# Causal self-attention in a decoder layer: the far corner of the transposed weights is moved by transfers, and its outputs contract over 128 keys

## The chip, the cores and the metric

The kernel runs on one core of a Trainium2 chip. The metric is device time in microseconds from launch to the last instruction, the median of three runs. The engines are TensorE (PE, with its weight loads shown apart as PEld), VectorE (DVE), ScalarE (ACT), GpSimd (POOL) and SyncE (SP), which here only issues DMA transfers.

## What is computed

A decoder layer on `x` of shape (2, 1024, 256) in fp32, with a layer norm after each of three parts: causal self-attention with 16 heads of 64 and rotary positions, cross-attention to a context of 77 tokens, and a feed-forward part that a router gives half of the tokens. The change concerns the first.

```python
q, k, v = rope(split(x @ Wq)), rope(split(x @ Wk)), split(x @ Wv)
sim  = einsum('bid,bjd->bij', q, k) * 64**-0.5
attn = softmax(where(tril, sim, -inf), axis=-1)
out  = einsum('bij,bjd->bid', attn, v)          # joined over heads, then @ Wo + bo
x    = layernorm(x + out)
# cross-attention, layernorm; gated feed-forward, layernorm
```

## The kernel before

**Tiling.** The 1024 tokens are `NT = 8` tiles of 128, and `NH = 4` is half of them. Two heads of 64 make a pair (`j` = 0, 1), and 2 batches times 8 pairs give 16 objects of class `Pair`. A score tile has 128 queries on the partitions and up to 1024 keys along the row, the causal part alone. Query tiles are worked in five groups, `(3, 1, 0), (4, 2), (5,), (6,), (7,)`.

**Steps of a pair**, named by letters in a hand-written order: `P` projections and `E` their copies out of PSUM; `d` (swap by DMA through `begin`, L219), `c`, `s`, `a` the rotation of half of the tokens, on POOL; `w` writes v to DRAM and `l` brings it back; `S` scores of a group (L342); `T` scale, mask and minimum on DVE (L355); `X` the exponentials on ACT (L363); `R` the transposes on DVE (L372); `Q`, `I`, `D`, `B` the inverse sums, sent through DRAM and spread along the row (`over`); `V0` to `V7` the outputs, one step per key tile (L410); `O` copies of the outputs out of PSUM (L424, for the last pair L430 with the scaling); `M` the scaling on POOL (L433); `W` the store. A step like `R41` is group 4, head 1.

**Transposes and outputs.** DVE transposes within blocks of 32 x 32. After step `R`, partition 32r + i of `p_t` holds key i of a block of 32, for the queries 32r to 32r + 31 of a tile: the partitions of quarter r still belong to query quarter r, and only the 32 partitions within a quarter run over keys. An output matmul can therefore contract only over 32 keys at a time: for key tile n, key block k of 4, head j and quarter r it takes 32 rows of `v4` (v arranged so that each partition quarter holds all keys in blocks of 32) and 32 rows of `p_t`, and adds into `po[r]`. Four quarters by two heads make eight tiles of 32 x 64 that work side by side in the array. Key tile n has 8 - n query tiles, so the columns of a matmul fall from 256 (V0) to 32 (V7).

**v.** `kept` copies both halves of v into one tile, `spread` writes all eight token tiles to `v_d` in DRAM, and `copies` reads them back into `v4` four times, once per quarter, on the queues of SP and ACT.

**Order.** TensorE, VectorE and ScalarE follow the order of three lists: `opening`, the periodic `steps` and `ending`. In a steady period the outputs of one pair lie among the scores of the next: `R40`, `S0`, `V0`, `V1`, `S1`, `V2` to `V4`, `S2`, `V5` to `V7`, `S3`. Scores have two PSUM buffers of two banks, one per head of a group, so `S` of a group waits for `T` of the group before it. SP issues in the order in which the text calls `begin`. After `V1` and `V7` the next `begin` waits for that output's last matmul (`gate`). Transfers from SP and ACT share eight completion semaphores in turn, and a transfer waits until the one eight places before it has landed.

**Pieces.** `split` cuts some projections into four column pieces and some scores into two, as many per pair as the list `pieces` allows. What is computed does not depend on it.

**Constants** (`causal`, `ones`, `earlier`, `b2`, `w_r`) are made or loaded at the start or after a `W` and kept throughout. `ones`, `earlier`, `b2` and `w_r` are used in the router and feed-forward part.

Of the kernel before, what the change touches and what calls it, by code (L numbers as in the profile page):

```python
# [8 lines left out]
F32 = mybir.dt.float32  # L9
# [7 lines left out]
P, R32 = 128, 32  # L17
B, T, C = 2, 1024, 256
H, D = 16, 64
# [3 lines left out]
NT = T // P  # L23
# [7 lines left out]
MASKED = -1e30  # L31
# [3 lines left out]
def decoder_layer(  # L35
# [23 lines left out]
    nc = tc.nc  # L59
    V, A, G, TE = nc.vector, nc.scalar, nc.gpsimd, nc.tensor  # L60

    const = ctx.enter_context(tc.tile_pool(name="const", bufs=1))
# [3 lines left out]
    dram = ctx.enter_context(tc.tile_pool(name="dram", bufs=2, space=DRAM))  # L66
# [14 lines left out]
    causal = const.tile([P, P], F32)  # L81
    make_causal_mask(nc, causal, MASKED)
    neg_half = const.tile([P, 1], F32)
    G.memset(neg_half, -0.5)
    ones = const.tile([P, P], F32)
    G.memset(ones, 1.0)
    earlier = const.tile([P, P], F32)
    make_upper_triangular(nc, earlier, diag=False)
# [42 lines left out]
    b2 = const.tile([P, C], F32)  # L131
    b_r = const.tile([P, 1], F32)
    b1 = const.tile([P, NF], F32)
    w_r = const.tile([P, C], F32)
# [7 lines left out]
    K4 = T // R32  # L142
    early = ctx.enter_context(ExitStack())
    e1 = early.enter_context(tc.tile_pool(name="early1", bufs=1, side="right"))
    e2 = early.enter_context(tc.tile_pool(name="early2", bufs=2, side="right"))
    with (
# [9 lines left out]
        fence = s1.tile([P, T], F32, name="fence")  # L156
        G.memset(fence[:, : T - P], 0.0)
        G.tensor_copy(fence[:, T - P :], causal)
        wo = s1.tile([P, NP, C], F32, name="wo")

        p_t = s1.tile([P, (NT + 1) * NT, P], F32, name="pT")
# [4 lines left out]
        def load(t, src):  # L166
            return lambda: nc.sync.dma_start(t, src)


        def load_next(h):  # L170
            if h == 0:
# [10 lines left out]
            3: [load(b2, L0_ffn_b2.partition_broadcast(P)), load(b_r, L0_ffn_b_r.partition_broadcast(P))],  # L182
            4: [
                load(w_r, L0_ffn_w_r.rearrange("c o -> (o c)").partition_broadcast(P)),
# [7 lines left out]
        NH = NT // 2  # L192
# [24 lines left out]
        def begin(dst, src):  # L217

            ins = nc.sync.dma_start(dst, src)  # L219
            if gate:  # L220
                tc.add_manual_dep(ins.ins, gate.pop().ins.name, after, reason="the outputs' instructions come first")
# [6 lines left out]
        pieces = [2, 1, 13, 13, 11, 10, 11, 12, 13, 12, 8, 9, 8, 8, 9, 0]  # L228
# [17 lines left out]
        class Pair:  # L246
# [61 lines left out]
            def kept(self, n):  # L308
                if self.v is None:
                    self.v = e1.tile([P, NT, P], F32, tag="v", name="v")  # L310
                    self.v_d = dram.tile([4, R32, NT * P], F32, tag="v", name="v_d")
                A.copy(self.v[:, n : n + NT // 2, :], self.pp["v", n])

            def spread(self):

                begin(self.v_d.rearrange("r k e -> (r k) e"), self.v.rearrange("p n d -> p (n d)"))

            def copies(self):

                self.v4 = s1.tile([P, K4, P], F32, tag="v4", name="v4")  # L320
                for r in range(4):
# [46 lines left out]
            def turn(self, g, j):  # L368
                for t, span in self.spans[g]:
                    first = (t, NT * (t + 1))[j]  # L370
                    step = (NT, 1)[j]
                    V.transpose(  # L372
                        p_t[:, first : first + t * step + 1 : step, :],
                        self.p[g, j][:, span].rearrange("p (n k) -> p n k", k=P),
                    )

# [22 lines left out]
            def output(self, n):  # L399
                if n == 0:  # L400
                    self.po = [ring.tile([P, NT, R32], F32, tag="t", name="po_self") for _ in range(4)]
                for k in range(4):
                    for j in range(2):
                        first = (NT * n + n, NT * (n + 1) + n)[j]
                        step = (1, NT)[j]
                        last = first + (NT - 1 - n) * step + 1

                        for r in range(k if n == NT - 1 else 0, 4):
                            rows = slice(r * R32, (r + 1) * R32)
                            ins = TE.matmul(  # L410
                                self.po[r][j * D : (j + 1) * D, n:, :],
                                self.v4[rows, NT * k + n, j * D : (j + 1) * D],
                                p_t[rows, first:last:step, k * R32 : (k + 1) * R32],
                                start=(n == 0 and k == 0), stop=(n == NT - 1 and k == r),
                            )
                if n in (1, NT - 1) and self.n < len(keys) - 1:
                    gate[:] = [ins]
                elif n == NT - 1:
                    final[:] = [ins]
# [20 lines left out]
        class Closing:  # L440
# [51 lines left out]
            ("Eq0", 1), ("Ek0", 1), ("Ev4", 1), ("Eq1", 1), ("a0", 0), ("R40", -1), ("S0", 0), ("T00", 0), ("T01", 0),  # L492
# [21 lines left out]
            "S": lambda a, x: a.scores(int(x)),  # L514
            "T": lambda a, x: a.least(int(x[0]), int(x[1])),
# [17 lines left out]
            0X31 0R20 1s0 0R30 0R21 1a0 2Eq1 0T40 3L 2Pv4 0T41 2Pv0 0X40 0X41 2Ek0 0R31 0R40 2Pq0 2Ev4 1S0 0R41 1T00  # L533
            2Eq0 2Ev0 0V0 1T01 0V1 2d0 0V2 1S1 1T11 0V3 1X00 0V4 0V5 1T10 1S2 1X01 1X11 1R00 0V6 0V7 2w 1X10 0O0 1T20
            1T21 1S3 1R10 1R01 0O1 2c0 1l 1X20 1T31 2Pk1 0O3 1T30 0O2 3Pv4 0Q 2Ek1 1S4 2c1 1X30 2s0 1X21 3Pq1 1R20 3Ev4
            3Pv0 2a0 1R11 3Pk0 0I 1T41 2d1 1R30 1X31 3Pq0 1T40 2S0 1R21 1X41 1X40 1R31 1R40 0D 1R41 2T00 3Ek0 2s1 3Eq1
# [7 lines left out]
            14S4 15Ek1 14T40 12W 4C 14T41 14X41 13O2 14R10 15a0 15d1 14R31 13O3 14R30 13D 14X40 15c1 14R40 14R41 15S0 4Y  # L544
# [3 lines left out]
            6U 15R41 15V0 4Z 14B 5Y 15V1 15V2 0f 15V3 14M 1f 7C 15V4 15V5 5Z 6Y 15V6 6Z 15D 15V7 15B 2f 15O1 15O3 7U 0n  # L548
# [8 lines left out]
        done, last = set(), len(keys) - 1  # L557
# [106 lines left out]
    def pool(name, bufs, **more):  # L664
        return ctx.enter_context(tc.tile_pool(name=name, bufs=bufs, reuse_waits="tile", **more))

    c1 = pool("cross1", 1)
# [5 lines left out]
    vo_d = dram.tile([B, HS, C], F32, tag="vo", name="vo_d", bufs=1)  # L673

# [86 lines left out]
    rows = out.rearrange("b t c -> (b t) c")  # L761
# [253 lines left out]
    with tc.manual_schedule(engines={TE.engine, V.engine, A.engine}):  # L1015
        first = Prepare()
# [139 lines left out]
```

## Time and profile before

| | us |
|---|---|
| median of 3 runs | 810.68 |
| lowest and highest run | 808.66, 815.99 |
| the profiled execution | 809.84 |
| its span, first to last instruction | 808.07 |
| self-attention with its rotation, from 51 to 526 of the span: PE busy | 462.7 of 475.0 |
| in that stretch DVE, ACT, POOL busy | 355.5, 254.1, 243.0 |
| 590 to 750 (cross-attention): PE busy | 159.4 of 160.0 |

The profile is one execution. A group line names the source line, engine and operation, then out<-in with their shapes and the count; then busy time, the mean in ns of one, and the idle time just before it with what ended that. A timeline line has start, length, line and operation, and in brackets the idle time before it. In a stage window the stretch comes first, then its length and each engine's busy time. PE's matmuls in fp32 run in two passes, so one matmul of the program is two rows of the trace. The granted clock of PE was 0.998 over the span.

### The profile page before, as it was taken

The numbers are of one execution on the slowest core, as the hardware profiler recorded it, in microseconds if no ns is written. First come the engines' busy times: TensorE is split into PE (matmuls) and PEld (weight loads), VectorE is DVE, ScalarE is ACT, GpSimd is POOL, SyncE is SP. The second block draws the span as 40 slices with busy tenths as digits, with TensorE's granted clock in tenths as the row PEclk, the third lists the DMA queues.
The fourth block names the chain that finished last, engine by engine and source line by source line (L and its number), as shares of the span: only waits on it lengthen the run. The fifth ranks groups of instructions, "written<-read, shape, count | busy, mean of one in ns | idle before, by whom it ended". The sixth has DMA issues, their size and how long they took to land.

```text
span 808.1 us, 26591 instructions
## 1 busy us (share of the span) xinstructions
PE 781.5 (97%) x11428; PEld 622.0 (77%) x11428; DVE 581.9 (72%) x1345; ACT 355.4 (44%) x842; POOL 367.7 (45%) x261
## 2 busy tenths in 40 slices
PE   8999999999999999999999988999999999999986
PEld 5565888888888888788788776688788888886745
DVE  2578678868778868678667796535577788888674
ACT  2565565655565556454554544102433332333130
POOL 2634455555375565365473553222033222261664
PEclk9999999999999999999999999999999999999999
DMA  5455477557567567668366467690450000011221
GB/s 195 129 148 177 129 210 209 171 168 211 157 169 230 158 179 223 174 171 204 112 198 185 133 185 158 173 324 3 168 187 1 1 1 0 1 53 53 68 91 52
DMA packets 65328, 112.32 MB, mean 139 GB/s; under 512 B 6497, under 2 KB 43707, under 8 KB 65211
## 3 DMA queue, kind: packets, MB, share of 16 engines
q1 hardware_dynamic: 59067, 89.64, 37.6%
q10 hardware_dynamic: 4608, 16.78, 7.5%
q0 software_dynamic: 1536, 4.20, 1.4%
q8 instruction: 90, 1.47, 0.8%
q14 instruction: 27, 0.22, 0.1%
HBM read 71.24 MB, written 22.59 MB: 116 GB/s over the span
## 4 chain that ended last, share of the span: by engine, by line
PE 82%; DVE 7%; POOL 4%; issue 4%; ACT 1%; DMA 1%; POOLq 0%; SPq 0%; ACTq 0%; DVEq 0%
PE po_self L410 17%; PE ps_scores L342 16%; PE pp_kq L268 13%; PE pp_v L303 7%; PE po_cross L998 6%; PE ps_cross L946 6%; PE po_proj L477 6%; PE pp_h L889 3%; PE po_ffn L900 2%; PE pt_p L978 1%; DVE pT L372 1%; DMA turned<-raw 1%; POOL comp L831 1%; POOL e L967 1%; DVE p L355 1%
## 5 line engine op out<-in xcount | busy, mean ns | idle before, releaser
L363 ACT ACTIVATE p<-p,neg 128x768 f32<-128x768 f32 (+7 forms) x256 | 196.3, 768 | 162.9 <-DVE neg L355 161.3
L355 DVE CUSTOM_DVE_ANT_0 p<-ps_scores,fence 128x512 f32<-128x512 f32 (+7 forms) x256 | 179.4, 750 | 104.9 <-PE ps_scores L342 104.5
L372 DVE STREAM_TRANSPOSE pT<-p 128x512 f32<-128x512 f32 (+7 forms) x256 | 175.7, 740 | 6.2 <-PE po_self L410 3.0
L410 PE MATMUL po_self<-pT,v 32*64 32x256 f32 (+6 forms) x7808 | 157.6, 295 | 10.1 <-issue 7.2
L410 PEld LDWEIGHTS po_self<-pT,v 32*64 32x64 f32 x7808 | 137.2, 130 | 34.9 <-issue 25.4
L342 PE MATMUL ps_scores<-kq 64*128 64x256 f32 (+3 forms) x1060 | 148.9, 411 | 1.8 <-DVE neg L355 1.0
L342 PEld LDWEIGHTS ps_scores<-kq 64*128 64x128 f32 x1060 | 93.3, 186 | 42.7 <-issue 28.2
L268 PE MATMUL pp_kq<-xT,w_pair 128*128 128x256 f32 (+2 forms) x524 | 118.6, 379 | 1.1 <-ACT xT L203 0.7
L291 POOL TENSOR_TENSOR turned<-turned,sin 128x1024 f32<-128x1024 f32 x31 | 73.2, 2362 | 93.0 <-DMA turned<-raw 80.1
L288 POOL TENSOR_TENSOR kq<-raw,cos 128x1024 f32<-128x1024 f32 x31 | 73.6, 2374 | 84.4 <-ACT raw L276 84.4
L268 PEld LDWEIGHTS pp_kq<-xT,w_pair 128*128 128x128 f32 x524 | 88.3, 190 | 23.9 <-issue 10.4
L967 POOL TENSOR_TENSOR e<-e,inv 128x616 f32<-128x616 f32 x32 | 38.2, 1215 | 113.0 <-DVE inv L966 67.2
L120 POOL TENSOR_TENSOR rs<-ve,neg_half 128x1 f32<-128x1 f32 x48 | 27.2, 570 | 107.2 <-DVE ve L118 105.2
L295 POOL TENSOR_TENSOR kq<-kq,turned 128x1024 f32<-128x1024 f32 x31 | 73.5, 2371 | 1.4
L998 PE MATMUL po_cross<-packed,pT 128*128 128x256 f32 (+1 forms) x320 | 72.5, 380 | 0.1
L946 PE MATMUL ps_cross<-wqk,x1T 128*128 128x308 f32 x256 | 69.2, 423 | 0.0
L998 PEld LDWEIGHTS po_cross<-packed,pT 128*128 128x128 f32 (+1 forms) x320 | 60.0, 190 | 9.4 <-ACT pT L984 0.3
L303 PEld LDWEIGHTS pp_v<-w_pair,xT 128*128 128x128 f32 x512 | 61.1, 192 | 4.0 <-issue 2.5
L303 PE MATMUL pp_v<-w_pair,xT 128*128 128x128 f32 x512 | 62.2, 275 | 0.0
L946 PEld LDWEIGHTS ps_cross<-wqk,x1T 128*128 128x128 f32 x256 | 47.4, 190 | 16.2 <-issue 0.7
L959 ACT ACTIVATE e<-e 128x616 f32<-128x616 f32 x32 | 23.0, 717 | 80.8 <-DVE e L955 80.8
L477 PE MATMUL po_proj<-wo,attnT 128*128 128x256 f32 x224 | 51.4, 381 | 0.3 <-ACT out_pair L424 0.3
(128 smaller groups left out, 817.0 us busy)
## 6 DMA issues: line engine op xcount, KB each, us to landing
turned<-raw SPq DMA_DIRECT2D x64, 256.0 KB, 4.7
v<-v_d ACTq DMA_DIRECT2D x32, 512.0 KB, 6.2
v<-v_d SPq DMA_DIRECT2D x32, 512.0 KB, 11.1
v_d<-v SPq DMA_DIRECT2D x16, 512.0 KB, 4.6
over<-inv_d SPq DMA_DIRECT2D x32, 256.0 KB, 4.8
attn_d<-out_pair SPq DMA_DIRECT2D x14, 512.0 KB, 4.3
attnT<-attn_d SPq DMA_DIRECT2D x8, 512.0 KB, 5.4
vo_d<-vo SPq DMA_DIRECT2D x2, 1232.0 KB
```

The lines of the kernel that those rows point to most:

```text
L268: TE.matmul(pp[:, cols], self.w[:, c, "kq".index(of), :], x_ts[self.b, n][:, c, cols], start=(c == 0), stop=(c == NC - 1),)
L288: E.tensor_tensor(self.kq[:, :, n * NB : (n + 1) * NB], self.raw[n], self.twice(cos, n), ALU.mult)
L295: E.tensor_tensor(dst, dst, self.turned[n], ALU.add)
L303: TE.matmul(pv[:, i, :], x_ts[self.b, 2 * n // NT][:, c, toks], self.w[:, c, 2, :], start=(c == 0), stop=(c == NC - 1),)
L342: TE.matmul(self.ps[j][:, cols], self.kq[rows, 1, t * P : (t + 1) * P], self.kq[rows, 0, cols.start - at : cols.stop - at], start=True, st ...
L355: V.tensor_tensor_reduce(p[:, span], self.ps[j][:, span], fence[:, T - (t + 1) * P :], -SCALE, -MASKED, ALU.add, ALU.min, neg[:, i : i + 1],)
L363: A.activation(p[:, span], p[:, span], AF.Exp, bias=neg[:, i : i + 1], scale=-1.0, accum_out=self.sums[:, j, t : t + 1],)
L372: V.transpose(p_t[:, first : first + t * step + 1 : step, :], self.p[g, j][:, span].rearrange("p (n k) -> p n k", k=P),)
L410: ins = TE.matmul(self.po[r][j * D : (j + 1) * D, n:, :], self.v4[rows, NT * k + n, j * D : (j + 1) * D], p_t[rows, first:last:step, k * R ...
L477: TE.matmul(self.po, of, wo[:, c, :], start=(c == 0), stop=(c == NP - 1))
L946: TE.matmul(ps[:, g, : Q * S], self.x_t[:, c, :], wqk[:, c, self.b, h : h + Q, :].rearrange("p h s -> p (h s)"), start=(c == 0), stop=(c = ...
L998: TE.matmul(po, self.p_t[:w, k, :], packed[self.b][:w, k, :], start=(k == 0), stop=(k == NK - 1))
```

## The change

`p_t` is laid out by key block of 32 first, so that the transposes of a tile go to four places with runs of 32 elements. A new step `J` comes after the last transposes of a pair: 16 transfers copy the weights of key tiles 4 to 7 and query tiles 4 to 7 (the far corner: under a causal mask key tiles 4 to 7 have no other queries) into `far`, such that partition quarter k gets key block k of every query quarter r. There the 128 partitions are 128 keys. The outputs V4 to V7 then contract over 128 keys at once: 8 matmuls of 128 rows by 64 columns per key tile, which take v directly from the copy of the projection (`self.v[NH]`), in place of 32 of 32 rows (20 for V7). Only key tiles 0 to 3 of v go through DRAM. `pieces` is zero for all pairs after the first. `causal` is made in place in `fence`; `ones`, `earlier`, `b2` and `w_r` move to the cross-attention stage.

```diff
-        pieces = [2, 1, 13, 13, 11, 10, 11, 12, 13, 12, 8, 9, 8, 8, 9, 0]
+        pieces = [2, 0, 0, 0, 0, 0, 0, 0, 0, 0, 0, 0, 0, 0, 0, 0]
...
-    K4 = T // R32
+    K4 = T // R32 // 2
...
-        p_t = s1.tile([P, (NT + 1) * NT, P], F32, name="pT")
+        p_t = s1.tile([P, 4, (NT + 1) * NT, R32], F32, name="pT")
+        far = s1.tile([P, 4, NT // 2 + 1, NT // 2, R32], F32, name="far")
...
             def kept(self, n):
                 if self.v is None:
-                    self.v = e1.tile([P, NT, P], F32, tag="v", name="v")
-                    self.v_d = dram.tile([4, R32, NT * P], F32, tag="v", name="v_d")
-                A.copy(self.v[:, n : n + NT // 2, :], self.pp["v", n])
+                    self.v = {}
+                self.v[n] = e1.tile([P, NH, P], F32, tag=f"v{n}", name="v", bufs=(1, 3)[n // NH])
+                A.copy(self.v[n], self.pp["v", n])
...
             def spread(self):
-                begin(self.v_d.rearrange("r k e -> (r k) e"), self.v.rearrange("p n d -> p (n d)"))
+                self.v_d = dram.tile([4, R32, NH * P], F32, tag="v", name="v_d")
+                begin(self.v_d.rearrange("r k e -> (r k) e"), self.v[0].rearrange("p n d -> p (n d)"))
...
                     V.transpose(
-                        p_t[:, first : first + t * step + 1 : step, :],
-                        self.p[g, j][:, span].rearrange("p (n k) -> p n k", k=P),
+                        p_t[:, :, first : first + t * step + 1 : step, :].rearrange("p c n q -> p n c q"),
+                        self.p[g, j][:, span].rearrange("p (n c q) -> p n c q", c=4, q=R32),
                     )
+
+            def joined(self):
+                for k in range(4):
+                    for r in range(4):
+                        begin(
+                            far[k * R32 : (k + 1) * R32, r, :, :, :].rearrange("p m t q -> p m (t q)"),
+                            p_t[r * R32 : (r + 1) * R32, k, NH * NT :, :].rearrange("p (m t) q -> p m (t q)", t=NT)[:, :, NH * R32 :],
+                        )
...
             def output(self, n):
...
+                if n < NH:
+                    for k in range(4):
+                        for j, cols in enumerate(heads):
+                            for r in range(4):
+                                rows = slice(r * R32, (r + 1) * R32)
+                                ins = TE.matmul(
+                                    self.po[r][cols, n:, :], self.v4[rows, NH * k + n, cols],
+                                    p_t[rows, k, across(j, n, NT), :], start=(n == 0 and k == 0), stop=False,
+                                )
+                else:
+                    for r in range(4):
+                        for j, cols in enumerate(heads):
                             ins = TE.matmul(
+                                self.po[r][cols, n:, :], self.v[NH][:, n - NH, cols],
+                                far[:, r, :, :, :].rearrange("p m t q -> p (m t) q")[:, across(j, n - NH, NH), :],
+                                start=False, stop=(n == NT - 1),
                             )
...
-            ("Eq0", 1), ("Ek0", 1), ("Ev4", 1), ("Eq1", 1), ("a0", 0), ("R40", -1), ("S0", 0), ("T00", 0), ("T01", 0),
+            ("Eq0", 1), ("Ek0", 1), ("Ev4", 1), ("Eq1", 1), ("a0", 0), ("R40", -1), ("J", -1), ("S0", 0), ("T00", 0), ("T01", 0),
...
-            6U 15R41 15V0 4Z 14B 5Y 15V1 15V2 0f 15V3 14M 1f 7C 15V4 15V5 5Z 6Y 15V6 6Z 15D 15V7 15B 2f 15O1 15O3 7U 0n
+            6U 15R41 15J 15V0 4Z 14B 5Y 15V1 15V2 0f 15V3 14M 1f 7C 15V4 15V5 5Z 6Y 15V6 6Z 15D 15V7 15B 2f 15O1 15O3 7U 0n
...
+    ones = c1.tile([P, P], F32, name="ones")
+    G.memset(ones, 1.0)
+    earlier = c1.tile([P, P], F32, name="earlier")
+    make_upper_triangular(nc, earlier, diag=False)
+    b2 = c1.tile([P, C], F32, name="b2")
+    w_r = c1.tile([P, C], F32, name="w_r")
+    nc.sync.dma_start(w_r, L0_ffn_w_r.rearrange("c o -> (o c)").partition_broadcast(P))
+    nc.sync.dma_start(b2, L0_ffn_b2.partition_broadcast(P))
```

`J` stands in the other two lists likewise, after `R41` of its pair.

## The prediction

> **What bounds the kernel now.** I read the busy times and the costliest groups first. PE is busy for nearly the whole span, and its largest line is the output matmuls of self-attention, L410.
>
> ```profile
> PE 781.5 (97%) x11428; PEld 622.0 (77%) x11428; DVE 581.9 (72%) x1345; ACT 355.4 (44%) x842; POOL 367.7 (45%) x261
> L410 PE MATMUL po_self<-pT,v 32*64 32x256 f32 (+6 forms) x7808 | 157.6, 295 | 10.1 <-issue 7.2
> ```
>
> The share is an average, so next comes PE's timeline of one steady period. Pairs of heads follow each other every 29.8 us (in the chain of waits the first score blocks start at 259.37 and 289.20). The order is S0, V0 V1, S1, V2 V3 V4, S2, V5 V6 V7, S3 and then projections.
>
> ```profile
> 259.30 1.80 PE L342 MATMUL ps_scores<-kq 64*128 64x256 f32 x20
> 261.03 3.50 PE L410 MATMUL po_self<-pT,v 32*64 32x256 f32 x128
> 264.46 2.00 PE L342 MATMUL ps_scores<-kq 64*128 64x512 f32 x12
> 266.38 3.03 PE L410 MATMUL po_self<-pT,v 32*64 32x192 f32 x146
> 269.59 0.96 PE L410 MATMUL po_self<-pT,v 32*64 32x128 f32 x46 [0.17 <-issue]
> 270.48 1.56 PE L342 MATMUL ps_scores<-kq 64*128 64x512 f32 x8
> 271.97 2.65 PE L410 MATMUL po_self<-pT,v 32*64 32x96 f32 x168
> 274.55 1.79 PE L342 MATMUL ps_scores<-kq 64*128 64x256 f32 x16
> ```
>
> Blocks follow without a gap: whatever PE saves here comes off the period until something else ends last. V5 to V7 need 2.6 us although they stream only 192 columns per position; V0 and V1 stream 480 in 3.43 us. The narrow outputs are bound by the number of instructions. Over nine middle blocks and eight last ones, the stage windows of L410 sum to:
>
> ```profile
> sum 33.92, PE 33.57 PEld 30.40; mean PE 3.73 PEld 3.38
> sum 20.21, PE 19.14 PEld 18.14; mean PE 2.39 PEld 2.27
> ```
>
> So V2 to V4 cost 33.92/9 = 3.77 us per pair, V5 to V7 20.21/8 = 2.53, together 6.30.
>
> Third, DVE's timeline of the same period, for what becomes late next.
>
> ```profile
> 254.55 3.23 DVE L372 STREAM_TRANSPOSE pT<-p 128x768 f32<-128x768 f32 x3
> 269.14 2.34 DVE L372 STREAM_TRANSPOSE pT<-p 128x512 f32<-128x512 f32 x6
> 272.07 0.96 DVE L355 CUSTOM_DVE_ANT_0 p<-ps_scores,fence 128x768 f32<-128x768 f32 x1 [0.59 <-PE ps_scores L342]
> ```
>
> The last transpose of a pair, R40, ends at 257.78. Before T2 (272.07) DVE idles only 0.59 us, and from there to 287.40 it is 99% busy (15.26 of 15.33 us); the next R40 ends 29.8 later, at 287.6.
>
> **The change, part by part.**
>
> *Outputs.* V0 and V1 keep form and 3.43 us: 16 sets of eight tiles, 8 x 480 = 3840 column times, 0.89 ns each. V2 and V3 keep form: 8 x 352 x 0.89 = 2.51 us. V4 to V7 fall from 212 matmuls in two passes (two rows of the trace each) to 32, two side by side: 8 x (128 + 96 + 64 + 32) x 0.89 = 2.28 us if streaming bounds them. No row shows 128 x 64 weights with so few columns. Below, streaming: 2.28. Above, each couple costs what one 128 x 128 matmul over 128 columns costs, 1.78 us per 16 in the chain of waits = 0.111: 32 x 0.111 = 3.55. I floor a couple at half of that, 0.055, since four transposes with 77 weight columns start within 526.30 to 526.62, 0.08 each, so a load for 64 columns should take less. This lifts only V7: 2.28 + 8 x 0.027 = 2.5. One more change of tile shape, from V3 to V4: blocks S1 (1024 columns, 2.00 us) and S2 (768, 1.56) give 1.72 ns per column and 0.24 us besides for a way in and out; I take 0.2 (bounds 0 and 0.24). V2 to V7 after: 2.51 + 2.5 + 0.2 = 5.2, saving 1.1 us per pair (bounds 0.0 and 1.5).
>
> The Trainium skill, "TensorE: Matmul & The Clock Gate", section "LDWEIGHTS (loading the stationary operand)", gives columns / 1.2 ns whatever the rows: 53 ns per half, and if two halves load one after the other a couple never goes below 107 ns. By that the sum would be the upper bound and the gain gone; eight 32 x 64 tiles (two halves per row group) pass in 0.214 us in V0 and V1, too slow to tell.
>
> *What stays of it.* S3 must wait for T2 (two score buffers). DVE is free of R00 and R01 at 271.48; T2 takes 1.76 (272.07 to 273.83), so S3 cannot start before 273.25, against 274.55: at most 1.3 us of the period can go. 1.1 fits; a gain of 1.5 would be cut.
>
> *The transfers (step J).* Sixteen transfers of 32 partitions x 5 runs of 512 B (80 KB) go out on SP after R40 and ahead of V0. Cover: V0 to V3 with S0 and S1. V4 starts at 266.38 + 2.51 = 268.9, 11.1 us after R40; DVE gains only 0.59 of PE's 1.1, so 10.6 remains, and 11.25 for the fourth quarter, wanted 0.65 later. Issue: SP's opening transfers start at 0.73, 1.22 and so on, the tenth at 5.29: 0.51 apart. The last is out 15 x 0.51 = 7.6 us after R40. Landing, SBUF to SBUF, in the answer for tile `turned`:
>
> ```profile
> DMA to landing us min/median/max: 2.2/4.7/8.9
> ```
>
> Best: 7.6 + 2.2 + 0.1 = 9.9. Worst in ordinary terms: there are eight completion semaphores, so the ninth transfer waits for the first; with the median 4.7 and 0.58 per issue (turned x2 takes from 264.74 to 265.90 in the fence below) the last goes out at 4.7 + 7 x 0.58 = 8.8 and lands at 13.5. I take about 10.3: the engines are free there (DMA share 0.05 from 261.0 to 264.5), and 1.3 MB at the 279 GB/s of 245 to 258 us takes 4.7 us. So J is hidden with some 0.9 us to spare.
>
> The skill's "DMA: Bandwidth & Descriptors", section "Rules for kernel authors", speaks against it: under 64 KB one pays mostly overhead, small transfers should be joined into one; its fixed 2 us per transfer would land the last at 9.6, also inside.
>
> *Queued behind J on SP.* The next step there is the swap for the rotation.
>
> ```profile
> 257.78 0.37 SPq L167 DMA_DIRECT2D wo<-in_L_attn_Wo_dram  x1
> 264.74 1.11 SPq L219 DMA_DIRECT2D turned<-raw  x2
> 265.90 1.25 SPq L219 DMA_DIRECT2D over<-inv_d  x2
> ```
>
> J holds SP until 257.8 + 8.2 = 266.0: swap and inverses go 1.3 us later. POOL's sine follows at 270.87 and its scaling ends at 275.55, with nothing on POOL until 280.28: 4.7 us hide it.
>
> *Halved v.* v_d and its copies lose 1.25 MB per pair; while they ran the engines were full (share 0.98). The copies land earlier, V0 does not wait for them now: nothing saved. *DVE.* The same transposes now write runs of 32 elements. Groups at L372 mix outputs in one run and with a stride at one mean each (128x512 692 ns, 128x1024 1198); I take 0. Bound: fixed part twice (two rows give 0.14 us) x 16 = 2.2 us per pair; nothing shows a gain. R10 also waits until J has read; it runs at 273.83, J is in by 268.1. *Unsplit matmuls.* Three projections as 24 quarter or half pieces take 5.38 us, 1.79 each; four whole matmuls take 1.72 to 1.91: 0. *Moved constants.* SP is idle from 539.4 to 571.97 and POOL from 556.6 to 584.73: the loads of w_r and b2 and three POOL fills fit; uncovered, under 2 us.
>
> *The last pair.* No later period hides J there, and the inverses queue behind it.
>
> ```profile
> 511.72 1.09 SPq L219 DMA_DIRECT2D over<-inv_d  x2
> 512.90 0.54 SPq L219 DMA_DIRECT2D attnT<-attn_d  x1
> 513.54 0.49 SPq L219 DMA_DIRECT2D inv_d<-inv  x1
> 519.68 1.09 SPq L219 DMA_DIRECT2D over<-inv_d  x2
> 526.14 1.42 DVE L430 TENSOR_TENSOR out_pair<-po_self,over 128x256 f32<-128x256 f32 x4 [4.54 <-PE po_self L410]
> ```
>
> R ends at 512.08. With J first, the first `over` goes at 520.3, inv_d at 522.1, the second `over` 6.1 later (513.54 to 519.68 now) at 528.2, landing by its median 4.8 at 533, where the scaling now starts at 526.14. PE's first projection after it can run seven eighths of its 3.46 us before. It starts at about 531.5 instead of 526.62: +5 us (bounds 3 and 7). At the head, pair 0 reaches V4 about 8 us after its transposes: +1.5 (0 to 2.5).
>
> **Sum.** The profiled execution took 809.84 us (span 808.07). 809.84 - 15 x 1.1 + 5 + 1.5 = 799.8; it lies 0.84 under the median of the runs, 810.68, so I say 801. From the ends of gain and costs, J hidden: 793 to 806.
>
> **Rivals.**
> - *J comes late (slower).* A wait at V4 replaces the instructions. From R40, the period closes as J's effective time (last landing less 0.65) + 0.96 (V4 and its shape change) + 1.59 (S2 to T2) + 15.5 (T2 to R40). That equals today's 29.8 at 11.75, a last landing at 12.4 us; above that the kernel loses. For it: the 4.7 us median, and DMA engines full until 261. Against: that backlog halves. At 13.5 each pair loses 1.1: 809.84 + 16.5 + 6.5 = 833; just over break-even 816.
> - *J partly late* (last landing 11.5 to 12.3): 0.1 to 0.8 of the gain per pair stays, 804 to 815.
> - *Weights bind the couples:* gain 0, the ends stay: 816.
> - *Slower transposes:* 15.3 us of DVE work grow by up to 1.7; little gain stays: about 811.
>
> **Numbers.** J hidden 0.50, partly late 0.12, late 0.27, weights 0.06, transposes 0.05. One per cent is about what a measurement can tell from no change: 802.6 and 818.8. Hidden gives 0.42 of faster and 0.08 of same; partly late 0.12, half of weights and most of transposes same, with 0.05 of late: 0.33; the rest slower: 0.25. Range 793 to 825: it leaves out about 0.05 below and 0.13 above.
>
> **What would show it.** PE's timeline: V4 right behind V3 without a DMA releaser, V5 to V7 in 1.7 us, periods near 28.7 us; SP: sixteen issues 0.51 apart; at the end PE idle some 5 us before the first po_proj from `over`. Wrong if V4 shows waits for `far`, if V5 to V7 stay at 2.5 us, or if the L372 groups grow.

## The result, and the profile after

| | median, us | runs | ratio to before |
|---|---|---|---|
| before (same session) | 813.34 | 808.66 to 817.08 | |
| after | 862.99 | 858.27 to 867.26 | 1.0612 (1.0524 to 1.07) |

The change costs 6%; the forecast was 801 us, in a range of 793 to 825. The profiled execution took 861.31 us (span 859.5). First its page: busy times, the granted clock in 40 slices, the chain of waits by engine, the new group of far matmuls, and the far transfers.

```profile
PE 797.3 (93%) x8188; PEld 558.3 (65%) x8188; DVE 578.0 (67%) x1345; ACT 353.6 (41%) x842; POOL 366.6 (43%) x260
...
PEclk9999899999999999999999998979999999999999
...
PE 42%; DVE 24%; SPq 19%; DMA 6%; issue 5%; POOL 3%; ACT 1%; POOLq 0%; DVEq 0%; ACTq 0%
...
L422 PE MATMUL po_self<-far,v 128*64 128x32 f32 (+3 forms) x1024 | 60.6, 263 | 36.4 <-DMA far<-pT 35.8
...
far<-pT SPq DMA_DIRECT2D x256, 80.0 KB, 2.2
```

PE has 3240 matmul rows fewer and is busy for 93% instead of 97%; its mean granted clock is 0.973 (0.998 before). The end of the span no longer hangs on PE alone: a fifth of the chain is SP's queue, all of it at L211, where `begin` issues transfers. Ahead of the far matmuls PE stood still 35.8 us in all until far transfers landed. Next PE's timeline of one middle period, the counterpart of the one shown of before.

```profile
284.18 3.50 PE L415 MATMUL po_self<-pT,v 32*64 32x256 f32 x128
287.61 2.00 PE L335 MATMUL ps_scores<-kq 64*128 64x512 f32 x12
289.54 2.67 PE L415 MATMUL po_self<-pT,v 32*64 32x192 f32 x128
292.13 0.44 PE L422 MATMUL po_self<-far,v 128*64 128x128 f32 x4
294.33 1.24 PE L422 MATMUL po_self<-far,v 128*64 128x128 f32 x12 [1.76 <-DMA far<-pT]
295.50 1.56 PE L335 MATMUL ps_scores<-kq 64*128 64x512 f32 x8
296.99 1.78 PE L422 MATMUL po_self<-far,v 128*64 128x96 f32 x48
```

V5 to V7 (last row) take 1.78 us where they took 2.65: the saving is there. But V4 stops after its first query quarter and waits 1.76 us for `far`; its last twelve rows take 1.24 us, where e_none below needs 1.09 for all sixteen, because the last quarter waits once more, shortly: its first row starts at 295.13. Three answers say why: SP's queue in the same pair; the answer for tile `far` in the window 281 to 296 (durations as minimum, median, maximum in ns; first and last start; then the idle time of PE and of its weight loads, PEld, ahead of the far matmuls); and one line of the DMA queues from 281.48 to 293.59 (queue, packets, MB, share).

```profile
281.48 12.11 SPq L211 DMA_DIRECT2D far<-pT  x16
293.75 1.16 SPq L211 DMA_DIRECT2D turned<-raw  x2
```

```profile
L211 SPq DMA_DIRECT2D far<-pT x16: 601/602/1694, 281.5 to 291.9; - x16
...
  DMA far<-pT: 4.4, 4
...
DMA to landing us min/median/max: 2.1/2.1/3.7
```

```profile
q8 instruction: 2, 0.03, 1.3%
```

SP needs 12.1 us to get the sixteen transfers out, where the forecast had the last one out after 7.6. Most issues hold the queue 602 ns, with 44 ns to the next. Two are longer, the tenth with 1.21 us and the last, begun at 291.9, with 1.69 us. SP's list of waits has no wait for a far transfer, so these two did not wait for an earlier landing. Each overlaps one of the two packets of the queue `q8 instruction`; more on that under e_half and e_twelve. The next view is DVE's timeline: the transposes R40 and R41 that J waits for, T2, and the next pair's R40 and R41 behind a reciprocal and more transposes left out here.

```profile
278.24 3.21 DVE L365 STREAM_TRANSPOSE pT<-p 128x768 f32<-128x768 f32 x3
...
297.09 0.96 DVE L348 CUSTOM_DVE_ANT_0 p<-ps_scores,fence 128x768 f32<-128x768 f32 x1 [2.46 <-PE ps_scores L335]
...
309.21 3.21 DVE L365 STREAM_TRANSPOSE pT<-p 128x768 f32<-128x768 f32 x3
```

The loop can be added up from these rows. R40 and R41 end at 281.45; the last wait for `far` ends 13.68 later (295.13); the rest of V4 takes 0.37, S2 and the way to T2 1.59, T2 to the end of the next R41 15.33. The sum is 30.97 us, and the next V0 starts 30.98 after this one (315.16). Before it was 29.8. DVE now idles 2.46 us before T2, where it idled 0.59.

At the end of self-attention PE stands still until the scaling of the last pair, which needs the inverses (`over`), and these queued behind the last J. First PE's row (the first projection of the second batch), then SP's queue.

```profile
577.39 2.93 PE L488 MATMUL po_proj<-wo,attnT 128*128 128x256 f32 x6 [9.52 <-DVE out_pair L441]
```

```profile
552.91 10.89 SPq L211 DMA_DIRECT2D far<-pT  x16
563.84 1.24 SPq L211 DMA_DIRECT2D over<-inv_d  x2
...
565.76 0.54 SPq L211 DMA_DIRECT2D inv_d<-inv  x1
571.93 1.09 SPq L211 DMA_DIRECT2D over<-inv_d  x2
```

Where the 50.8 us up to that projection come from (577.39 against 526.62), by starts of V0: pairs 0 to 4 took 169.5 us against 149.7 (19.7 more), pairs 5 to 8 126.1 against 119.6 (6.5), pairs 9 to 14 205.3 against 190.5 (14.7), the rest lies after V0 of pair 15 (25.6 against 15.6: 10).

### The profile page after: what moved, and what is told of

Its sections match the earlier page's. It is cut to its first block, busy times and chain, and to the rows that moved or that the text cites. A ratio compares the mean times of both kernels' runs of the same rounds, so it can differ in the third digit from the quotient of the medians.

```text
span 859.5 us, 20440 instructions
## 1 busy us (share of the span) xinstructions
PE 797.3 (93%) x8188; PEld 558.3 (65%) x8188; DVE 578.0 (67%) x1345; ACT 353.6 (41%) x842; POOL 366.6 (43%) x260
## 4 chain that ended last, share of the span: by engine, by line
PE 42%; DVE 24%; SPq 19%; DMA 6%; issue 5%; POOL 3%; ACT 1%; POOLq 0%; DVEq 0%; ACTq 0%
SPq L211 19%; DVE pT L365 11%; DVE p L348 7%; PE ps_scores L335 6%; PE po_cross L1018 6%; PE ps_cross L966 6%; PE po_proj L488 5%; PE po_self L422 3%; DMA far<-pT 3%; PE pp_kq L260 3%; PE pp_h L909 3%; DMA over<-inv_d 3%; PE po_ffn L920 2%; PE pp_v L295 1%; PE pt_p L998 1%
## 5 line engine op out<-in xcount | busy, mean ns | idle before, releaser
L335 PE MATMUL ps_scores<-kq 64*128 64x512 f32 (+3 forms) x768 | 160.8, 530 | 0.3 <-POOL kq L287 0.3
L260 PE MATMUL pp_kq<-xT,w_pair 128*128 128x512 f32 (+1 forms) x264 | 117.6, 587 | 0.8 <-ACT xT L195 0.8
L335 PEld LDWEIGHTS ps_scores<-kq 64*128 64x128 f32 x768 | 75.1, 195 | 58.5 <-issue 45.8
L415 PE MATMUL po_self<-pT,v 32*64 32x224 f32 (+3 forms) x4096 | 100.1, 338 | 2.7 <-DVE pT L365 2.1
L415 PEld LDWEIGHTS po_self<-pT,v 32*64 32x64 f32 x4096 | 84.5, 131 | 18.4 <-issue 7.6
L422 PE MATMUL po_self<-far,v 128*64 128x32 f32 (+3 forms) x1024 | 60.6, 263 | 36.4 <-DMA far<-pT 35.8
L260 PEld LDWEIGHTS pp_kq<-xT,w_pair 128*128 128x128 f32 x264 | 47.7, 190 | 56.1 <-issue 41.5
L422 PEld LDWEIGHTS po_self<-far,v 128*64 128x64 f32 x1024 | 45.2, 148 | 58.2 <-issue 33.1
L295 PEld LDWEIGHTS pp_v<-w_pair,xT 128*128 128x128 f32 x512 | 61.7, 192 | 14.7 <-issue 10.3
```

The source lines that it names most:

```text
L260: TE.matmul(pp[:, cols], self.w[:, c, "kq".index(of), :], x_ts[self.b, n][:, c, cols], start=(c == 0), stop=(c == NC - 1),)
L295: TE.matmul(pv[:, i, :], x_ts[self.b, 2 * n // NT][:, c, toks], self.w[:, c, 2, :], start=(c == 0), stop=(c == NC - 1),)
L335: TE.matmul(self.ps[j][:, cols], self.kq[rows, 1, t * P : (t + 1) * P], self.kq[rows, 0, cols.start - at : cols.stop - at], start=True, st ...
L415: ins = TE.matmul(self.po[r][cols, n:, :], self.v4[rows, NH * k + n, cols], p_t[rows, k, across(j, n, NT), :], start=(n == 0 and k == 0), ...
L422: ins = TE.matmul(self.po[r][cols, n:, :], self.v[NH][:, n - NH, cols], far[:, r, :, :, :].rearrange("p m t q -> p (m t) q")[:, across(j, ...
```

## The experiments

Two theories. One: only J is late, because one queue issues its sixteen transfers too slowly; PE's wait at V4 then closes the loop above. Two: something else in the change is dear, be it the uncut matmuls, the strided transposes, the mere presence of the transfers, or the clock. All figures in one table: "J" is the median time from the first far issue of a pair to the end of its last, on all queues; the periods are those of pairs 6 to 8, from V0 to V0; "V0 of 15" and "po_proj" are the starts of the last pair's V0 and of the first projection of batch 1 in the profiled run (for e_twelve it was the slowest of ten, 819.5 us). The kernel before ran beside each group, with medians of 812.6 to 814.3 us.

| run | J, us | periods, us | V0 of 15 | po_proj | median, us | ratio to before (95%) |
|---|---|---|---|---|---|---|
| before | - | 29.6 to 29.8 | 511.0 | 526.6 | 813.3 | |
| after | 12.3 | 31.0 to 32.9 | 551.8 | 577.4 | 863.0 | 1.0612 (1.0524 to 1.07) |
| e_none | - | 28.6 | 497.0 | 512.1 | 797.4 | 0.9794 (0.9752 to 0.9837) |
| e_nowait | 12.5 | 28.6 | 500.3 | 526.7 | 814.7 | 1.0013 (0.9971 to 1.0055) |
| e_half | 5.8 | 28.6 | 496.8 | 518.5 | 802.4 | 0.9866 (0.983 to 0.9902) |
| e_twelve | 9.0 | 28.6 to 32.2 | 511.6 | 534.7 | 813.7 | 0.9995 (0.9964 to 1.0027) |
| e_queues | 7.7 | 28.6 to 30.9 | 518.5 | 541.2 | 826.2 | 1.0162 (1.0122 to 1.0201) |
| e_late | 12.3 | 28.4 to 30.5 | 510.9 | 538.0 | 824.5 | 1.0148 (1.0095 to 1.0201) |
| e_busy | 12.7 | 33.0 | 561.1 | 588.2 | 874.9 | 1.0788 (1.0754 to 1.0823) |
| e_busy9 | 12.4 | 30.9 to 35.3 | 551.2 | 577.2 | 861.9 | 1.0585 (1.0537 to 1.0632) |
| e_tail | 12.3 | 30.5 to 33.8 | 551.8 | 571.1 | 853.1 | 1.0514 (1.0468 to 1.056) |
| e_best | 9.7 | 28.8 to 31.0 | 523.6 | 538.8 | 818.6 | 1.0075 (1.0045 to 1.0104) |
| e_win12 | 9.9 | 28.4 to 28.5 | 497.7 | 515.6 | 798.3 | 0.9799 (0.9751 to 0.9846) |
| e_win | 8.3 | 28.4 | 496.0 | 511.7 | 797.3 | 0.9813 (0.9766 to 0.9861) |

**e_none: the change without its transfers.** J is gone from all lists, and V4 to V7 read the mask tile.

```diff
-far[:, r, :, :, :].rearrange("p m t q -> p (m t) q")[:, across(j, n - NH, NH), :],
+fence[:, : (NH + 1) * NH * R32].rearrange("p (m q) -> p m q", q=R32)[:, across(j, n - NH, NH), :],
```

> The changed kernel without step J: V4 to V7 read a constant tile (the mask) in place of `far`, so the far corner of the weights is left out of the outputs; the form and number of all PE and DVE instructions stay. Theory 1 (only J is late: sixteen issues at 0.65 us plus stalls plus 2.2 us of landing stand between R40 and V4): steady period 28.5 to 28.8 us, no dip of the granted clock in the pairs, about 795 to 800 us. Theory 2 (something else in the change is dear: the matmuls that are no longer cut in pieces, the transposes' new stride, the halved v): stays at 830 or above. Between, the part that remains above 800 belongs to theory 2.

797.4 us: theory one. The window over four middle pairs (columns: window, its length, PE busy and instructions, granted clock, DMA share, GB/s) shows PE without a gap at full clock, and PE's timeline prices the far matmuls and S3.

```profile
195.00:312.00 117.00, 117.00 (x1689) 1.00 0.49 146
```

```profile
260.22 2.67 PE L415 MATMUL po_self<-pT,v 32*64 32x192 f32 x128
262.82 1.09 PE L422 MATMUL po_self<-fence,v 128*64 128x128 f32 x16
263.84 1.56 PE L335 MATMUL ps_scores<-kq 64*128 64x512 f32 x8
265.33 1.79 PE L422 MATMUL po_self<-fence,v 128*64 128x96 f32 x48
267.05 2.05 PE L335 MATMUL ps_scores<-kq 64*128 64x512 f32 x8
```

Period 28.6, 1.1 us under the mean of the same three periods before (29.7). The uncut matmuls, the transposes with runs of 32 and the halved v together cost nothing that the period would show.

**e_nowait: the transfers without the wait.** The same read of the mask tile, J issued as in the changed kernel.

> J's sixteen transfers are issued as in the changed kernel, but V4 to V7 read the constant tile, so PE never waits for them (the far corner is left out of the outputs). Theory 1 (PE's wait for `far` is what costs): steady periods as without J, 28.5 to 28.8 us; what is lost lies at the end, where the swaps and inverses queue behind J: 803 to 815 us. Theory 2 (the transfers cost by being there: SP blocked for 12 us, swap and inverses late, DMA engines shared): 840 us or more, with PE's or POOL's idle time before `turned` or `over` in each period.

814.7 us, at the upper end of theory one. The steady period is 28.6 us with all sixteen transfers in it: J's presence delays nobody there, the later swap and inverses included. What it costs, 17.3 us against e_none, is mostly at the end: the first projection starts 14.6 us later, of which 3.4 us lie ahead of V0 of the last pair and 11.2 behind it. PE's row there says for whom it waits.

```profile
526.67 3.78 PE L488 MATMUL po_proj<-wo,attnT 128*128 128x256 f32 x8 [12.70 <-DVE out_pair L441]
```

So of the 65.6 us between e_none and after, 48.3 go when PE no longer waits for `far`, and 17.3 remain, most of them from the queue behind J. The 48.3 are more than the 35.8 us of PE's idle time; what the rest is made of is not shown.

**e_half and e_twelve: the dose.** Eight, then twelve transfers in place of sixteen (two and three rounds of the loop over k; the lines are those of e_half).

```diff
-                for k in range(4):
+                for k in range(2):
                     for r in range(4):
...
+        G.memset(far[2 * R32 :, :, :, :, :], 0.0)
```

> Eight transfers in place of sixteen (key quarters 0 and 1; rows 64 to 127 of `far` stay zero, so a part of the far corner is left out). Theory 1: the last goes out 8 x 0.65 = 5.2 us after R40 and lands at 7.4, before V4 wants it at 10.6: no wait in the steady pairs, 28.5 to 28.8 us per period, half the loss at the end: 800 to 810 us. If instead each transfer costs the same wherever it lies (theory 2), half of the loss against no J stays: about 830.

> Twelve transfers in place of sixteen (key quarters 0 to 2; rows 96 to 127 of `far` stay zero, so a part of the far corner is left out). If J's lateness is (number) x 0.65 + stalls + 2.2: the last goes out 7.8 to 9 us after R40, landing at 10 to 11.2, where V4 asks at 10.6: waits of 0 to 0.6 us, steady periods 28.6 to 29.2, 806 to 818 us, much nearer the eight transfers (802) than the sixteen (863), since only what passes the break-even counts. If each transfer adds the same: 832.

802.4 and 813.7 us, both where theory one has them. The price per transfer is not constant: 0.6 us each for the first eight, 2.8 for the next four, 12 for the last four. That is the form of something hidden up to a break-even. J's own length has no such step: 5.8, 9.0 and 12.3 us are 0.73, 0.75 and 0.77 us per transfer. The answers for tile `far` tell how long PE and its weight loads stood idle before the far matmuls, and what ended it: after, e_twelve, e_half in this order (us, times; "issue" is idle time for which the profile shows no wait).

```profile
  DMA far<-pT: 60.7, 64
  issue: 33.1, 47
```

```profile
  issue: 17.2, 38
  DMA far<-pT: 14.9, 21
```

```profile
  issue: 9.4, 30
```

With sixteen transfers per pair 64 of these starts wait for `far`, with twelve 21, with eight none.

What makes J longer than 0.65 us per issue (602 ns and 44 ns to the next) are single long issues, at any place in the burst, among the first eight too: 31 of the 256 in after took more than 0.8 us, up to 2.0, and 14 of the 128 in e_half. In after, e_nowait, e_half and e_twelve SP's waits name no far transfer. But all 31 long issues of after overlap a packet of 16 KB of the queue `q8 instruction`, and end a median of 0.39 us after that packet does; of the other 225 issues 25 overlap one. In e_nowait 37 of 38 long issues do, in e_half 13 of 14. The page counts these packets, first after, then before:

```profile
q8 instruction: 65, 1.06, 0.6%
```

```profile
q8 instruction: 90, 1.47, 0.8%
```

Their number follows PE's instructions, matmuls and weight loads together: 16,376 in after and 22,856 before, and 18,936 with 75 packets in e_busy, so one packet to some 253 instructions. It looks as if PE's own program is brought in by them, and as if the transfer that SP is issuing is held up meanwhile. This rests on the coincidence; no run changed these packets alone.

**e_queues: two queues.** Every second transfer goes out on ACT's queue.

```diff
-                        begin(
+                        (begin, nc.scalar.dma_start)[r % 2](
```

> The sixteen transfers as they are, every second one issued by ACT's queue instead of SP's. Theory 1 (the issue rate of one queue): each queue needs 8 x 0.65 = 5.2 us, the last lands 7.4 to 8 us after R40, no wait in the steady pairs; SP is free 6 us sooner: 800 to 812 us. Theory 2 (the DMA engines or the landing limit J, not the issue): the last still lands 13 us or more after R40 and the time stays above 845. ACT's own work moves by 5 us per pair, and it is busy 44% of the span, so a loss of 0 to 1 us per pair there is possible.

826.2 us, above what was expected, for a reason that the theory had not named. With 7.7 us of J, and the same bytes and number of transfers, hardly a wait for `far` is left (5.4 us in all, against 35.8). The loss is mostly in the opening: the issues on ACT wait for R41, and behind them, in ACT's order, stand two evacuations that free PE's accumulators. ACT's timeline, then PE's, then a line of SP's waits (us in all, times, longest):

```profile
49.91 5.74 ACTq L374 DMA_DIRECT2D far<-pT  x8
55.70 0.58 ACT L268 COPY raw<-pp_kq 128x512 f32<-128x512 f32 x1 [6.46 <-DMA far<-pT]
```

```profile
56.33 6.90 PE L415 MATMUL po_self<-pT,v 32*64 32x256 f32 x188 [4.93 <-ACT raw L268]
```

```profile
SPq L211 <- DMA far<-pT: 11.7, 17, 2.1
```

Pair 0 took 41.9 us instead of the 29.4 of e_none; ahead of V0 of pair 1 PE stands still another 4.73 us, with ACT's copies again behind eight issues. The end lost 9.1 us to idle PE, much as in the changed kernel. Only in runs with two queues, which take the eight completion semaphores in turn, does SP wait for earlier far transfers. The Trainium skill, "DMA: Bandwidth & Descriptors", section "Issuing engines are not separate DMA queues", says that starting DMAs on several engines saves only the sequencer's time, which is usually small beside the DMA. This case's trace agrees that issue time is saved: J fell from 12.3 to 7.7 us. Small beside the DMA it is not here: one issue holds the queue 0.6 us and lands after 2.2, but the sixteen of a pair add up to 12 us. Whether the transfers run slower with both queues can't be told: the median landing was 2.8 us, and 2.2 to 2.7 in runs with one queue.

**e_late: the place of the wait.** V4 goes behind S2 of the next pair, where V5 stood already.

```diff
-            ("V3", -1), ("V4", -1), ("T11", 0), ("S2", 0), ("X00", 0), ("V5", -1), ("R00", 0), ("X01", 0), ("R01", 0),
+            ("V3", -1), ("T11", 0), ("S2", 0), ("V4", -1), ("X00", 0), ("V5", -1), ("R00", 0), ("X01", 0), ("R01", 0),
```

In the opening and ending lists V4 and V5 go behind S2 likewise.

> V4 and V5 stand behind S2 of the next pair in PE's order; transfers and instructions are the changed kernel's. So `far` is wanted 1.6 us later after R40 and S2 (and with it T2, the next link to R40) no longer waits for `far`. Theory 1 (the loop R40 - J - V4 - S2 - T2 - R40 sets the period): the loop is cut at S2; what remains of the wait (14.2 us after R40 for the last landing against 12.2 to 12.8) is PE's own, 1 to 2 us per pair: steady period 29.5 to 30 us instead of 30.9, 835 to 850 us, the end still 15 us longer than without J. If the loop does not run through S2 and T2: 860 or more.

824.5 us, less than expected. With nothing but PE's order changed, 38 us of the loss go: S2 no longer waits, and T2 follows DVE's transposes without a gap. What remains in the trace is PE's own wait for `far` in some pairs (9.2 us in all, 1.46 us in the worst middle one), and the end (10.56 us of idle PE).

```profile
240.37 1.71 PE L335 MATMUL ps_scores<-kq 64*128 64x512 f32 x8
243.54 1.11 PE L422 MATMUL po_self<-far,v 128*64 128x128 f32 x12 [1.46 <-DMA far<-pT]
```

**e_busy and e_busy9: the clock.** After some waits the granted clock falls. In the changed kernel's pair 1, V4 and V5 take 3.83 us after a wait; the same 32 rows take 1.75 us in e_none:

```profile
96.07 3.83 PE L422 MATMUL po_self<-far,v 128*64 128x128 f32 x32 [2.92 <-DMA far<-pT]
```

```profile
88.55 1.75 PE L422 MATMUL po_self<-fence,v 128*64 128x128 f32 x32
```

Here PE runs matmuls with zero weights ahead of V4, 20 couples, then 9.

```diff
+                    for j, cols in 20 * list(enumerate(heads)) if n == NH else ():
+                        TE.matmul(
+                            self.po[3][cols, n:, :], fence[:, :D], ident.rearrange("p (m q) -> p m q", q=R32),
+                            start=False, stop=False,
+                        )
```

> Ahead of V4, PE runs 40 extra matmuls with zero weights (20 couples over 128 columns, added to `po_self` as zeros), some 2.2 us in which the changed kernel idles for `far`. Theory 1a (part of the loss is the granted clock, which falls to 0.50 after PE's waits of 2 to 3 us): the clock stays near 1 in pairs 0 to 4 and 9 to 13 and their periods shorten by 1 to 3 us each: 840 to 855 us. Theory 1b (the clock's fall costs nothing, since PE waits anyway): within 3 us of the changed kernel or up to 10 above it (the steady pairs wait for `far` 1 to 3 us, so the extra work may stand out there).

> As the run with 40 zero-weight matmuls ahead of V4, with 18 of them. There the 20 couples took 4.59 us (0.23 each, two rows per matmul), 2.2 us more than PE's wait, so the period was PE's own 33.0 us; nine couples take 2.1 us and fit into the wait. Theory 1a (the fall of the granted clock after the wait lengthens the loop): the mean clock rises from 0.973 to 0.99, the first pairs' periods fall below 34 us, total 848 to 858. Theory 1b (it costs nothing): 861 to 868.

The first overshot:

```profile
293.43 4.59 PE L421 MATMUL po_self<-ident,fence 128*64 128x128 f32 x80
```

20 couples took 4.59 us, 0.23 each, as the forecast's 0.89 ns per column has it (2 x 128 columns) and not 0.11 as the expectation had it; they made PE the bound at 33.0 us. The second fits the wait. Windows of the changed kernel and of e_busy9 from 98 to 104 us (busy time of each engine; the third number from the right is the clock):

```profile
98.00:104.00 6.00, 6.00 (x61) 4.03 (x62) 1.25 (x3) 0.25 (x1) 2.29 (x1) 0.62 0.77 238
```

```profile
98.00:104.00 6.00, 5.74 (x70) 3.59 (x71) 2.67 (x6) 1.67 (x5) 1.01 (x1) 1.00 0.85 251
```

The clock stays at 1.00 and the total does not move (861.9 against 863.0; the intervals overlap). Pairs 0 to 4 took 4.4 us less (165.1 against 169.5), pairs 5 to 8 4.0 more. So keeping the clock up does not bring the loss back. What the clock's fall costs by itself is not measured, because the filler has a price of its own where a wait is shorter than its 2.1 us. The Trainium skill, "TensorE: Matmul & The Clock Gate", section "Why this matters for your kernels", warns of PE gaps above some 3 us; the gap here, 2.92 us, lies at that mark, and the clock fell behind it. It was still not the way to the time.

**e_tail: the queue at the end.** The `over` of pair 14 and the inverses of pair 15 go out ahead of the last J, pair 15's `over` on ACT's queue.

```diff
-                    begin(
+                    (nc.scalar.dma_start if self.n == len(keys) - 1 else begin)(
...
-... 2= 14D 15I 15R40
-            6U 15R41 15J 15V0 4Z 14B 5Y 15V1 15V2 0f 15V3 14M 1f 7C 15V4 15V5 5Z 6Y 15V6 6Z 15D 15V7 15B ...
+... 2= 14D 14B 15I 15D 15R40
+            6U 15R41 15J 15V0 4Z 5Y 15V1 15V2 0f 15V3 14M 1f 7C 15V4 15V5 5Z 6Y 15V6 6Z 15V7 15B ...
```

> Only the last two pairs' transfers change places: the inverses of pair 14 (`over`) and the store of pair 15's inverses go out ahead of pair 15's J, and pair 15's `over` is issued by ACT's queue. Theory (12.7 us of idle PE at the end are the inverses queued behind J on SP): the wait before the first po_proj of the second batch falls from 9.5 us to 1 to 4 us, total 6 to 10 us less: 853 to 857 us. If the wait there has another cause (attnT, the scaling): no change.

853.1 us, as expected. SP's order and PE's first projection:

```profile
550.21 1.09 SPq L211 DMA_DIRECT2D over<-inv_d  x2
551.39 0.53 SPq L211 DMA_DIRECT2D inv_d<-inv  x1
552.87 13.21 SPq L211 DMA_DIRECT2D far<-pT  x16
```

```profile
570.68 0.49 PE L635 MATMUL pt_cx<-ident,cx 77*128 77x77 f32 x4
571.14 2.83 PE L488 MATMUL po_proj<-wo,attnT 128*128 128x256 f32 x12
```

The 9.52 us of idle PE are gone; the projection follows the context's transposes at once. It starts only 6.25 us sooner, since V4 of pair 15 now waits 3.28 us for a J that took 13.2 us instead of 10.9.

**e_best, e_win12, e_win: parts together.** e_best issues J by query quarters (r outside, k inside, so that quarter r is whole after four transfers), quarters 0 to 2 on SP and 3 on ACT, ACT's share of pairs 0 and 1 behind the evacuations, and takes e_tail's end. e_win12 adds e_late. e_win is e_win12 with ten transfers on SP and six on ACT (eight and eight in pair 15 in both). The lines are those of e_win.

```diff
+            def joined(self, which, queue):
+                for i in which:
+                    r, k = divmod(i, 4)
+                    queue(
+                        far[k * R32 : (k + 1) * R32, r, :, :, :].rearrange("p m t q -> p m (t q)"),
...
+                    )
...
+            "J": lambda a, x: a.joined(range(8 if a.n == len(keys) - 1 else 10), begin),
+            "K": lambda a, x: a.joined(range(8 if a.n == len(keys) - 1 else 10, 16), nc.scalar.dma_start),
```

> J by query quarters (quarter r complete after four transfers), quarters 0 to 2 on SP, quarter 3 on ACT's queue (for pair 15 two and two), ACT's share of pairs 0 and 1 behind the evacuations that PE waits for; the end as in the run with the reordered inverses. Theory 1: SP's twelve issues take 7.8 us, landing 10.0 us after R40, before V4 asks at 10.6: steady period 28.6 us, opening within 3 us of the run without J, no wait at the end: 798 to 806 us. If the total number of transfers counts and not one queue's: 825 or more.

> Together: J by query quarters with twelve transfers on SP and four on ACT's queue, V4 and V5 behind S2, the inverses ahead of J at the end. The kernel with the split alone waited 1.1 to 3.1 us for the third quarter in nine pairs; S2 takes 1.56 us, so most of these waits go: steady periods 28.6 to 29.2 us, 800 to 810 us. If ACT's issues or the later V4 cost by themselves (S3 later, ACT's exponentials late): 812 or more.

> As the one before with ten transfers on SP and six on ACT's queue (eight and eight for the last pair): SP is done 1.3 us sooner, so no wait for `far` in the steady pairs: 28.6 us per period, 798 to 806 us; ACT's exponentials begin 1.3 us later, which costs where ACT's wait reaches R00 (batch 1): then no better than the one before.

e_best missed its figure: 818.6 us. In the pair whose V0 starts at 236.65 SP's twelve transfers went out over 10.4 us instead of 7.8: two issues took 1.03 and 1.73 us, and SP waited some 0.9 us for earlier landings. PE waited for the third quarter:

```profile
247.40 0.66 PE L420 MATMUL po_self<-far,v 128*64 128x128 f32 x8 [2.14 <-DMA far<-pT]
```

With V4 behind S2 such waits are covered: e_win12 (798.3) and e_win (797.3) came out just under their ranges. PE's timeline of e_win, one middle pair:

```profile
261.82 1.71 PE L335 MATMUL ps_scores<-kq 64*128 64x512 f32 x8
263.46 2.66 PE L420 MATMUL po_self<-far,v 128*64 128x128 f32 x64
```

V4 to V7 run as one block without a wait. e_win is 1.9% faster than before (0.9766 to 0.9861) and as fast as e_none, which has no transfers at all. Six and four transfers on ACT can't be told apart by time. Fewer and larger transfers were not tried.

## Why the prediction was wrong

- *Outputs: right.* V5 to V7 were forecast at 1.7 us and take 1.78. From start to start V2 to V4 and V5 to V7 take 3.62 and 1.72 us in e_none, 5.3 against a forecast of 5.2. The period fell by 1.1 us there, as the sum had it. (V4 to V7 had 116 matmuls before, not 212; the sum goes by columns and doesn't use the number.)
- *Weights, transposes, halved v: right.* With J away none of them shows. The rival of slower transposes is out: their mean is 739 ns in e_none, and 740 in the kernel before. *Unsplit matmuls* were put at 0; S3 takes 2.05 us where it took 1.79, and the period of e_none holds that.
- *The transfers: this step failed.* "SP's opening transfers start at 0.73, 1.22 and so on, the tenth at 5.29: 0.51 apart. The last is out 15 x 0.51 = 7.6 us after R40." The runs show 0.65 from issue to issue, and besides about one long issue in eight, 12.3 us in all. In the pair shown the wait for `far` ended 13.7 us after R40, against 9.9 in the sum: of the 3.8 us between, 2.1 are the interval (15 x 0.14) and 1.7 the two long issues. The interval came from transfers of another kind at the start of the kernel. The swap's 0.58, which stood in the same text, would have given 11.0, and the true 0.65 alone 12.0, both still inside the break-even at 12.4; the long issues, for which the sum had no term, carry it past. So "J is hidden with some 0.9 us to spare" fell. The landing, the other term, was right at its lower end: 2.2 us.
- *The upper end, 13.5, was met by luck.* It had the ninth transfer wait for the first to land, and a landing of 4.7 us. In the changed kernel no issue of J waits for a far transfer, and the landing is 2.2 us.
- *The law for the period: right in kind.* With the measured landing it gives 13.68 - 0.65 + 0.96 + 1.59 + 15.5 = 31.1; 30.97 was measured. It comes as close in pairs 4 and 8; in pairs 5 and 6 the period was 1.1 and 1.3 us longer than the law has it, and in pairs 9 to 12, whose periods were the longest before too (32.4 to 33.7), 3.4 to 4.7.
- *The rival "J comes late" was the case, and its price too small:* 833 us at a landing of 13.5, against 863 at about that. The opening was put at +1.5 us for pair 0, while pairs 0 to 4 cost 19.7 together. All of it goes with the wait (146.9 us for them in e_nowait, 149.7 before); how it divides between the earlier V4 of these pairs and the clock stays open. The end was put at +5 us; from V0 of the last pair to the projection it cost 10 us against before, and 11.2 in e_nowait against e_none: J held SP for 11 to 12 us there, not 8.2.
- *Swap and inverses behind J, hidden by POOL's 4.7 us: right* in the middle pairs (e_nowait, 28.6 us).
- The signs listed were the right ones: waits for `far` at V4, PE idle at the end from `over`.
- The Trainium skill's rule that the prediction sets against the change ("DMA: Bandwidth & Descriptors", section "Rules for kernel authors") speaks of transfers under 64 KB; those of J have 80 KB, and no run here tries another size. The 2 us per transfer that the prediction takes from the same page stand against a measured landing of 2.2 us; what was missing lay in the issues.

## What to carry to other kernels

Price a burst of transfers by the issue rows of its own kind, queue and stage, by the longest rows as well as the median, and multiply the error by the burst's length: 0.14 us per issue and two long issues in sixteen turned a spare microsecond into a loss of 50. Before a wait is put on the engine that bounds the kernel, write down the loop it closes and what is queued behind it; here moving V4 by one block was worth 38 us, as much as a second queue for the transfers (863.0 to 826.2). Look at both ends of the pipeline apart from its middle: a queue that is harmless in the steady state cost some 11 us where nothing followed to hide it.

## What the runs showed of the hardware

- A transfer of 80 KB inside SBUF (32 partitions x 5 runs of 512 B) holds SP's queue 602 ns, with 44 ns to the next; it lands 2.2 us after it is issued (median of after).
- About one such issue in eight is longer, up to 2.0 us. All 31 of more than 0.8 us in after overlap a 16 KB packet of the queue `q8 instruction`, of which there is one to some 253 PE instructions, and end about 0.39 us after it. That the packet holds the issue up is inferred from this.
- With one queue no issue of J waited for a far transfer to land (after, e_nowait, e_half, e_twelve); with two queues SP waited 17 times, 11.7 us in all (e_queues). Eight and eight took 7.7 us instead of 8 x 0.65 = 5.2 there, and twelve on SP beside four on ACT 10.4 instead of 7.8 in the pair of e_best above.
- A PE wait of 2.92 us, up to 96.07 us, was followed by a mean granted clock of 0.62 from 98 to 104 us; with zero-weight matmuls in the waits it stayed at 1.00, and the total stayed where it was.
